# Layer 0's attention with scores in runs of nine over a ring of seven PSUM banks

## The chip, the cores and the metric

The kernel runs on one core of one Trainium2 chip. The metric is device time in microseconds for one launch. Five engines work side by side, each through its own queue in order: TensorE (PE) multiplies, ScalarE (ACT) takes exponentials and copies, VectorE (DVE) adds, GpSimd (POOL) and SyncE (SP) issue most DMAs. PE's results go to PSUM, which has eight banks of 512 fp32 per partition.

## The reference

Two layers on an image batch `x` of 2 x 256 x 64 x 64 in fp32. Layer 0 is attention over all 4096 pixels with 8 heads of 32 channels; layer 1 (local and strided attention and a 3x3 convolution) is not touched by the change.

```python
B, C, H, W = (2, 256, 64, 64)
NUM_HEADS = 8
qkv = jnp.einsum('bchw,oc->bohw', x, qkv_w) + qkv_b[None, :, None, None]
qkv = qkv.reshape(b, 3, num_heads, head_dim, n)
q, k, v = (qkv[:, 0], qkv[:, 1], qkv[:, 2])
attn_logits = jnp.einsum('bhci,bhcj->bhij', q, k) * scale
attn_weights = jax.nn.softmax(attn_logits, axis=-1)
out = jnp.einsum('bhij,bhcj->bhci', attn_weights, v)
...
x = x + _L0_conv_ref(_gn(x), L0_conv_qkv_w, L0_conv_qkv_b, 8)
x = x + _L1_conv_ref(_gn(x), ...)
```

## The kernel before

For each of the two images the kernel normalises `x`, projects queries, keys and values, runs layer 0's attention (`attention0`), and then layer 1. Only `attention0` changes.

**Units, blocks, groups.** A head's queries are cut in two halves of four tiles of 512; half a head is a group, so there are 16 groups. In a group `j` runs over 32 blocks of 128 keys, and a block has four units, one for each query tile. A unit is a matmul of 128 keys by 512 queries into one PSUM bank (the score, L505), followed by an exponential from that bank into a place of `es` (L511). An image has 16 x 32 x 4 = 2048 units. No maximum is subtracted; the sum of the exponentials is divided out at the end.

**Places.** The exponentials go round a ring of `RING` = 28 places of 512, the first `RING_A` = 17 in one tile and the rest in another, so a run of units is cut where places 17 and 28 begin. `at_places` does the cutting.

**Values.** For a block, `quarters` (L521) multiplies four units by the block's values; each unit makes 32 of the 128 output partitions of bank `av`. A block is worked in two half-blocks of 256 queries, but in one step at `j` = 0 and `j` = 31, so a group has 62 steps (`per_group`). One matmul shows as two records in the trace: a half-block has eight.

**Sums of the exponentials.** DVE adds each block's four units into `e` (L550, L558), except seven blocks a group (`SUMMED`), which POOL adds with accumulating DMAs (L566, L568). At the group's end the sums are joined (L748) and reduced over partitions by PE into a spare PSUM bank (`sum_rows`, called in `finish`), copied by ACT (L598) and sent off by SP.

**The loop.** PE, ACT and DVE run in the order in which the program is written (`manual_schedule`). A round of the loop calls `scores`, which takes seven units in three PSUM tiles, `sa` of three banks, `sb` of two and `sc` of two, and writes one exponential for each tile. Then come value steps of units that were scored in earlier rounds: `have` is the number of units before this call, `share` keeps the steps two behind their even share, `must` is the least number of blocks that have to be begun so that the places that the next call overwrites are free. When somebody wants a spare bank (`wanted`), `scores` uses two banks of `sa` and gives the third away; the row sum is then made after two steps (`here == 2`). A group's end closes the round, and ACT copies `av` (L762) so that the next group can begin.

The eight banks are thus three of `sa`, two of `sb`, two of `sc` and one of `av`. A tile of several banks is free for the next round when its exponential has read all of it.

Of the kernel before, what the change touches and what calls it, by code (L numbers as in the profile page):

```python
# [9 lines left out]
F32 = mybir.dt.float32  # L10
I32 = mybir.dt.int32
F32R = mybir.dt.float32r
AF = mybir.ActivationFunctionType
# [4 lines left out]
P = 128  # L18
B, C, H, W = 2, 256, 64, 64
N = H * W  # L20
T = 512
# [4 lines left out]
NH0 = C // HD0  # L26
# [14 lines left out]
def direct_layers(ctx: ExitStack, tc: tile.TileContext, a: dict, out: bass.AP, bad: bass.AP):  # L41
# [3 lines left out]
    nc = tc.nc  # L45
# [11 lines left out]
    psum = {}  # L57

    def w4(shape, name, dtype=F32):
        return work.tile(shape, dtype, tag="w4", name=name)  # L60
# [304 lines left out]
    SC0 = 1.0 / math.sqrt(HD0)  # L365
# [8 lines left out]
    NJ = N // P  # L374
# [77 lines left out]
    RING, RING_A = 28, 17  # L452
# [11 lines left out]
    def attention0(b, xts, held):  # L464
# [10 lines left out]
        n_units = NH0 * 2 * NJ * 4  # L475
# [4 lines left out]
        places = []  # L480
        n_places = 0

        def at_places(first, n):

            while n > 0:
                at = first % RING
                m = min(n, (RING_A if at < RING_A else RING) - at)
                yield m, es[:, at : at + m, :] if at < RING_A else held["es"][:, at - RING_A : at - RING_A + m, :]
                first, n = first + m, n - m

        def scores(spare):

            nonlocal n_places
            bank = None
            for tag, size in (("sa", 3), ("sb", 2), ("sc", 2)):
                first = len(places)
                n = min(size - (spare and size == 3), n_units - first)
                if n <= 0:
                    break
                sc = psum["sc"].tile([P, size, T], F32, tag=tag, name=f"{tag}_{b}_{first}")  # L500
                if spare and size == 3:
                    bank = sc[:, size - 1, :]
                for i in range(n):
                    g, (j, u) = (first + i) // (4 * NJ), divmod((first + i) % (4 * NJ), 4)
                    nc.tensor.matmul(  # L505
                        sc[:, i, :], held["k", g // 2][:, j * P : (j + 1) * P], held["q", g, u // 2][:, u % 2, :],
                        start=True, stop=True,
                    )
                i = 0
                for m, dst in at_places(n_places, n):  # L510
                    nc.scalar.activation(dst, sc[:, i : i + m, :], AF.Exp, scale=SC0)  # L511
                    i += m
                places.extend(range(n_places, n_places + n))
                n_places += size
            return bank

        def quarters(dst, lhs, rhs, start, stop, part=None):

# [17 lines left out]
        def add_rows(g, j):  # L536
            if j == 0:
                sums[g] = psum["sc"].tile([P, T], F32, tag="av", name=f"av_{b}_{g}")
                added[g] = [w4([P, 2, T], f"e_{b}_{g}_{w}") for w in range(2)]
                return  # L540
            for w in range(2):
                dst = added[g][w]
                if j in summed(g):
                    if w == 0:
                        add_in_memory(g, j)
                    continue
                if j == 1:
                    first = two_units(g, 0, w), two_units(g, 1, w)
                    if len(first[0]) == len(first[1]) == 1:
                        nc.vector.tensor_add(dst, first[0][0][1], first[1][0][1])  # L550
                    else:
                        for s in range(2):
                            nc.vector.tensor_add(dst[:, s, :], unit(g, 0, 2 * w + s), unit(g, 1, 2 * w + s))
                    continue
                for s, src in two_units(g, j, w):
                    if g == last and j in SUMMED_LAST:
                        continue
                    nc.vector.tensor_add(dst[:, s, :], dst[:, s, :], src)  # L558
# [11 lines left out]
        def work_of(g, j):  # L570


            if (g, j) < (last, NJ - 3):
                add_rows(g, j)
            for part in (None,) if j in (0, NJ - 1) else range(2):
                if part == 1:
                    yield
                quarters(
                    sums[g], held["v"][:, (g // 2) % 2, j, :], lambda u: unit(g, j, u), j == 0, j == NJ - 1, part
                )  # L580

        def sum_rows(g, rows):
            if g == last:
                for part in range(2):
                    for j in SUMMED_LAST:
                        quarters(rows, ones, lambda u: unit(g, j, u), j == SUMMED_LAST[0], False, part)
                    quarters(rows, ones, lambda u: acc[u], False, False, part)
                    quarters(rows, ones, lambda u: added[g][u // 2][:, u % 2, :], False, True, part)
                return
            quarters(rows, ones, lambda u: added[g][u // 2][:, u % 2, :], True, True)  # L590
# [140 lines left out]
        def steps():  # L731

            for done in range(NH0 * 2 * NJ):
                g, j = divmod(done, NJ)
                if (g, j) == (last, NJ - 3):
                    assert len(places) == n_units
                    held["rows"] = psum["sc"].tile([P, 3, T], F32, tag="sa", name=f"rows_{b}")[:, 2, :]
                    for i in (NJ - 3, NJ - 2, NJ - 1):
                        add_rows(g, i)
                    sum_rows(g, held["rows"])  # L740
                for _ in work_of(g, j):
                    yield done
                if g and j == 0:

                    for w in range(2):
                        dst = added[g - 1][w]
                        for s in range(2) if w == 0 else (slice(0, 2),):
                            nc.vector.tensor_add(dst[:, s, :], dst[:, s, :], acc[s] if w == 0 else pair)  # L748
                    waiting.clear()
                if g and j == 1:  # L750
                    wanted.append(late[0].send)
                if g and j in (9, 17):
                    next(late[0])
                for what in also.get((g, j), ()):
                    what()
                if j == 4 and g % 2 == 0 and g // 2 + 1 < NH0:
                    fetch_head(b, g // 2 + 1, held)
                if j == NJ - 1:
                    waiting.append(g)
                    avs = w4([P, 2, T], f"avs_{b}_{g}")  # L760
                    if g < last:
                        nc.scalar.copy(avs[:, 0, :], sums[g])  # L762
                    copied[g] = avs
                    late[:] = [finish(g)]
                    next(late[0])
                    if g + 2 < NH0 * 2:
                        fetch_queries(b, g + 2, held)
                yield done + 1

        E = mybir.EngineType  # L770
        with tc.manual_schedule(engines={E.PE, E.Activation, E.DVE}):

            per_group = 2 * NJ - 2
            work, begun, taken = steps(), 0, 0
            scores(False)
            final = False
            while not final:
                have = len(places)  # L780
                use = wanted.pop(0) if wanted else None
                bank = scores(use is not None)
                final = have == n_units
                ready = have // 4
                share = have * per_group // (4 * NJ) - 2

                must = sum(place < n_places + 7 - RING for place in places[: 4 * ready : 4])
                if must % NJ == 1:
                    must += 1
                assert must <= ready  # L790
                here = 0
                while begun < ready and (taken < share or begun < must or final or use is not None):
                    if use is not None and here == 2:
                        use(bank)
                        use = None
                        continue
                    here += 1
                    group = begun // NJ
                    begun = next(work)
                    taken += 1  # L800
                    if begun // NJ > group and begun >= must and not final and use is None:
                        break
                if use is not None:
                    use(bank)
            assert next(work, None) is None
            return *finish_last(last), st
# [585 lines left out]
    for b in range(B):  # L1392
        xts = x_first if b == 0 else ahead["xts"]
        w0 = w0_first if b == 0 else ahead["w0"]
        with tc.tile_pool(name=f"ps0_{b}", bufs=8, space=PSUM) as psum["ps"]:
# [7 lines left out]
            held = project0(b, xn, w0)  # L1403
# [571 lines left out]
```

## Time and profile before

| what | value |
|---|---|
| runs | 3115.47, 3118.44 and 3122.96 us, median 3118.44 |
| profiled execution: span, first to last instruction | 3116.4 us |
| profiled execution: time around the span | not given in the profile |
| PE matmul busy | 3031.2 us, 97% |
| DVE busy | 2467.0 us, 79% |
| ACT busy | 2313.6 us, 74% |
| POOL busy | 836.7 us, 27% |
| attention0, first image: first score burst to last | 118.4 to 1151.0 us |
| attention0, second image | 1666.3 to 2699.3 us |

How to read the profile: a group is a line, an engine and an operation with the tiles that it writes and reads; the arrow points to what is written. Matmuls are pipelined and overlap in the trace, so the distance from start to start says more of their cost than their length. PEld is the load of a matmul's stationary operand. In the timeline, rows of one group that follow each other are merged and counted. A number in square brackets is idle time of the engine before the row, and what ended it.

### The profile page before, as it was taken

Reading aid. Unit: us, or ns where it says so; the run is one execution under the profiler, and the core shown is the slowest. Engines: PE = TensorE matmul, PEld = TensorE weight load, DVE = VectorE, ACT = ScalarE, POOL = GpSimd, SP = SyncE. Lnnn points to the kernel's source line nnn. Section 1 sums busy time; section 2 is a strip of 40 time slices with the busy share of each in tenths; the row PEclk is TensorE's granted clock in tenths of the full one; section 3 lists DMA queues with packets and bytes.
Section 4 is the critical chain, followed back from the end, with each engine's and each line's share of the span. In section 5 each row is a group of like instructions: output and inputs, shape, how many; then the busy total and the mean of one; then the engine's idle time right before and its main releaser. Section 6 shows DMA issues by size and latency. Waiting matters only on the chain. (4 is left out here: it accounts for less than half of the span.)

```text
span 3116.4 us, 62659 instructions
## 1 busy us (share of the span) xinstructions
PE 3031.2 (97%) x25129; PEld 1830.6 (59%) x25129; DVE 2467.0 (79%) x3126; ACT 2313.6 (74%) x2436; POOL 836.7 (27%) x923
## 2 busy tenths in 40 slices
PE   6999999999999999999989999999999999999998
PEld 4555555555555556677755555555555555476765
DVE  4599989999899999856556998989989999834543
ACT  2699999999999984622237999999999999734333
POOL 2022222222222231055301222222222222305440
PEclk9999999999999999999999999999999999999999
DMA  7969679797897761230159687796888975700000
GB/s 241 270 132 185 143 150 172 154 178 150 164 181 154 145 133 33 75 134 29 41 193 268 128 176 151 156 176 138 177 162 164 181 153 123 170 4 4 21 14 22
DMA packets 243787, 424.41 MB, mean 136 GB/s; under 512 B 99112, under 2 KB 109916, under 8 KB 241308
## 3 DMA queue, kind: packets, MB, share of 16 engines
q0 software_dynamic: 94992, 238.36, 39.8%
q1 hardware_dynamic: 147580, 181.68, 21.6%
q8 instruction: 199, 3.26, 0.4%
q14 instruction: 104, 0.85, 0.1%
q10 hardware_dynamic: 912, 0.27, 0.0%
HBM read 119.03 MB, written 68.39 MB: 60 GB/s over the span
## 5 line engine op out<-in xcount | busy, mean ns | idle before, releaser
L558 DVE TENSOR_TENSOR e<-e,es 128x1024 f32<-128x1024 f32 (+1 forms) x956 | 1038.6, 1142 | 79.6 <-ACT es L511 77.9
L521 PE MATMUL av<-es,v 128*32 128x256 f32 (+1 forms) x9644 | 746.7, 390 | 0.0
L558 DVE TENSOR_TENSOR e<-e,v 128x1024 f32<-128x1024 f32 (+1 forms) x640 | 675.2, 1107 | 47.7 <-ACT v L511 46.6
L511 ACT ACTIVATE es<-sa 128x1536 f32<-128x1536 f32 (+1 forms) x444 | 635.7, 1432 | 93.1 <-PE sa L505 54.9
L505 PE MATMUL sa<-q,k 128*128 128x512 f32 x1736 | 561.4, 430 | 9.2 <-ACT avs L598 3.5
L521 PE MATMUL av<-v 128*32 128x256 f32 (+1 forms) x6228 | 506.5, 389 | 0.0
L521 PEld LDWEIGHTS av<-es,v 128*32 128x32 f32 x9644 | 316.1, 109 | 299.4 <-issue 160.6
L505 PEld LDWEIGHTS sa<-q,k 128*128 128x128 f32 x1736 | 280.0, 188 | 291.8 <-issue 135.4
L505 PE MATMUL sc<-q,k 128*128 128x512 f32 x1180 | 371.4, 396 | 1.7 <-ACT es L511 0.7
L505 PE MATMUL sb<-q,k 128*128 128x512 f32 x1180 | 371.0, 395 | 1.1 <-ACT es L511 1.1
L521 PEld LDWEIGHTS av<-v 128*32 128x32 f32 x6228 | 216.5, 109 | 178.6 <-issue 81.2
L511 ACT ACTIVATE es<-sc 128x1024 f32<-128x1024 f32 x296 | 306.9, 1037 | 0.0
L511 ACT ACTIVATE v<-sc 128x1024 f32<-128x1024 f32 x294 | 304.9, 1037 | 0.1
L511 ACT ACTIVATE es<-sb 128x1024 f32<-128x1024 f32 x296 | 302.0, 1020 | 3.8 <-DMA acc<-es 3.8
L511 ACT ACTIVATE v<-sb 128x1024 f32<-128x1024 f32 x294 | 300.0, 1020 | 0.0
L505 PEld LDWEIGHTS sb<-q,k 128*128 128x128 f32 x1180 | 221.2, 188 | 55.4 <-ACT es L511 2.9
L505 PEld LDWEIGHTS sc<-q,k 128*128 128x128 f32 x1180 | 210.5, 188 | 71.8 <-ACT es L511 12.1
L511 ACT ACTIVATE v<-sa 128x1536 f32<-128x1536 f32 (+1 forms) x146 | 209.2, 1433 | 35.6 <-PE sa L505 17.0
L948 PE MATMUL mm<-v,wf 128*128 128x256 f32 x1024 | 227.6, 380 | 1.5 <-DVE z L957 1.5
L568 POOL DMA_DIRECT2D es<-es x116 | 98.9, 853 | 475.6 <-ACT es L511 424.3
L948 PEld LDWEIGHTS mm<-v,wf 128*128 128x128 f32 x1024 | 193.3, 190 | 36.8 <-issue 9.9
L938 POOL TENSOR_TENSOR v<-col 128x512 f32<-128x512 f32 x128 | 165.1, 1316 | 179.2 <-ACT rk_sr L1089 39.2
(262 smaller groups left out, 3179.0 us busy)
## 6 DMA issues: line engine op xcount, KB each, us to landing
acc<-es POOLq DMA_DIRECT2D x128, 512.0 KB, 6.2
acc<-v POOLq DMA_DIRECT2D x84, 512.0 KB, 6.4
es<-es POOLq DMA_DIRECT2D x136, 256.0 KB, 4.5
v<-es POOLq DMA_DIRECT2D x132, 256.0 KB, 5.1
k<-wk_halves SPq DMA_DIRECT2D x64, 512.0 KB
q<-wq_halves SPq DMA_DIRECT2D x256, 128.0 KB
v<-v POOLq DMA_DIRECT2D x90, 256.0 KB, 5.4
es<-v POOLq DMA_DIRECT2D x86, 256.0 KB, 3.9
```

What stands on the lines that cost most here:

```text
L505: nc.tensor.matmul(sc[:, i, :], held["k", g // 2][:, j * P : (j + 1) * P], held["q", g, u // 2][:, u % 2, :], start=True, stop=True,)
L511: nc.scalar.activation(dst, sc[:, i : i + m, :], AF.Exp, scale=SC0)
L521: nc.tensor.matmul(dst[HD0 * u : HD0 * u + HD0, n], lhs, rhs(u)[:, n], start=start, stop=stop)
L558: nc.vector.tensor_add(dst[:, s, :], dst[:, s, :], src)
L568: nc.gpsimd.dma_start(out=dst, in_=src, accum_op=ALU.add)
L938: (nc.gpsimd.tensor_add if plus else nc.gpsimd.tensor_sub)(dst, rows(one), rows(two))
L948: nc.tensor.matmul(mm[:, m, r, :], wf[:, k, 4 * r + q, m * P : (m + 1) * P], v[r // 2][:, r % 2, k, :], start=k == 0, stop=k == KC - 1,)
```

## The change

The three PSUM tiles become one tile `ring` of seven banks, and a unit's bank is its place modulo seven. A call of `scores` takes nine units in runs of 1, 1, 3, 2 and 2 (`PHASE`), each with its own exponential; a run is also cut where the ring of banks or the ring of places wraps. So the eighth and ninth unit of a call use the banks of the first and second. A spare bank is the next one of the ring, taken after the nine, and skips a place as before. `have` now counts the units that lie at least seven behind the end of the call just made. `reach`, ten, takes the place of seven in `must`. A group's last two steps are worked in the round that reaches them (`ending`), and the last three blocks of all are held until all scores are made. The row bank of the last group comes from the ring, too.

```diff
-        def scores(spare):
+        BANKS = 7
+
+        PHASE = (1, 1, 3, 2, 2)
+        ring = psum["sc"].tile([P, BANKS, T], F32, tag="ring", name=f"ring_{b}")
+
+        def spare_bank():
 
             nonlocal n_places
-            bank = None
-            for tag, size in (("sa", 3), ("sb", 2), ("sc", 2)):
-                first = len(places)
-                n = min(size - (spare and size == 3), n_units - first)
-                if n <= 0:
-                    break
-                sc = psum["sc"].tile([P, size, T], F32, tag=tag, name=f"{tag}_{b}_{first}")
...
+            n_places += 1
+            return ring[:, (n_places - 1) % BANKS, :]
+
+        def runs_of(n):
+
+            at = n_places
+            while n > 0:
+                e = at % RING
+                m = min(n, BANKS - at % BANKS, (RING_A if e < RING_A else RING) - e)
+                yield at, m
+                at, n = at + m, n - m
+
+        def scores():
+
+            nonlocal n_places
+            for size in PHASE:
+                for at, m in list(runs_of(min(size, n_units - len(places)))):
+                    sc = ring[:, at % BANKS : at % BANKS + m, :]
+                    for i in range(m):
...
+                    ((_, dst),) = at_places(at, m)
+                    nc.scalar.activation(dst, sc, AF.Exp, scale=SC0)
+                    places.extend(range(at, at + m))
+                    n_places = at + m
...
-                    held["rows"] = psum["sc"].tile([P, 3, T], F32, tag="sa", name=f"rows_{b}")[:, 2, :]
+                    held["rows"] = spare_bank()
...
+            behind, reach = 7, sum(PHASE) + 1
             work, begun, taken = steps(), 0, 0
-            scores(False)
-            final = False
-            while not final:
-                have = len(places)
+            while begun < NH0 * 2 * NJ:
+                scores()
                 use = wanted.pop(0) if wanted else None
-                bank = scores(use is not None)
-                final = have == n_units
-                ready = have // 4
+                bank = spare_bank() if use is not None else None
+                final = len(places) == n_units
+                have = n_units if final else len(places) - behind
+                ready = max(0, have) // 4
                 share = have * per_group // (4 * NJ) - 2
 
-                must = sum(place < n_places + 7 - RING for place in places[: 4 * ready : 4])
+                must = sum(place < n_places + reach - RING for place in places[: 4 * ready : 4])
...
-                while begun < ready and (taken < share or begun < must or final or use is not None):
+                while begun < ready:
                     if use is not None and here == 2:
                         use(bank)
                         use = None
                         continue
+                    ending = taken % per_group >= per_group - 2
+                    if not (taken < share or ending or begun < must or final or use is not None):
+                        break
+                    if not final and begun == NH0 * 2 * NJ - 3:
+                        break
```

More of the change, by code (lines that the diff above doesn't have):

```diff
@@ L489, in at_places @@
                 first, n = first + m, n - m
-        def scores(spare):
+        BANKS = 7
+        PHASE = (1, 1, 3, 2, 2)
+        ring = psum["sc"].tile([P, BANKS, T], F32, tag="ring", name=f"ring_{b}")
+        def spare_bank():
             nonlocal n_places
-            bank = None
-            for tag, size in (("sa", 3), ("sb", 2), ("sc", 2)):
-                first = len(places)
-                n = min(size - (spare and size == 3), n_units - first)
-                if n <= 0:
-                    break
-                sc = psum["sc"].tile([P, size, T], F32, tag=tag, name=f"{tag}_{b}_{first}")
[L501 to L515, printed above, removed]
@@ new lines, in spare_bank @@
+            n_places += 1
[13 more added lines that the diff above has]
+                    for i in range(m):
+                        unit = len(places) + i
+                        g, (j, u) = unit // (4 * NJ), divmod(unit % (4 * NJ), 4)
+                        nc.tensor.matmul(
+                            sc[:, i, :], held["k", g // 2][:, j * P : (j + 1) * P], held["q", g, u // 2][:, u % 2, :],
+                            start=True, stop=True,
+                        )
+                    ((_, dst),) = at_places(at, m)
+                    nc.scalar.activation(dst, sc, AF.Exp, scale=SC0)
+                    places.extend(range(at, at + m))
+                    n_places = at + m
```

## The prediction

> **What bounds the kernel now.** I read the 40 slices first, then the busy time of the two stretches that the change lives in, then single rows of PE and ACT in them.
>
> ```profile
> PE   6999999999999999999989999999999999999998
> DVE  4599989999899999856556998989989999834543
> ACT  2699999999999984622237999999999999734333
> ```
>
> ```profile
> 118.40:1151.00 1032.60, 1027.90 (x10029) 584.73 (x10029) 946.83 (x967) 966.51 (x915) 276.23 (x338) 1.00 0.80 162
> 1666.30:2699.30 1033.00, 1027.79 (x10030) 584.12 (x10030) 947.07 (x967) 966.34 (x915) 272.70 (x338) 1.00 0.80 161
> ```
>
> Columns of the second view: stretch, us, then busy time of PE, weight loads, DVE, ACT, POOL. These are layer 0's attention for the two images: 1033 us each, two thirds of the span. PE has work in 99.5% of it, ACT in 94%, DVE in 92%. A busy PE says little by itself, so I look at how PE's time is made up. Two rounds of the loop in PE's timeline (start, duration, group):
>
> ```profile
> 602.91 0.98 PE L505 MATMUL sa<-q,k 128*128 128x512 f32 x3
> 603.73 0.63 PE L505 MATMUL sb<-q,k 128*128 128x512 f32 x2
> 604.20 0.62 PE L505 MATMUL sc<-q,k 128*128 128x512 f32 x2
> 604.75 1.50 PE L521 MATMUL av<-es,v 128*32 128x256 f32 x24
> 606.18 0.96 PE L505 MATMUL sa<-q,k 128*128 128x512 f32 x3
> ...
> 634.80 0.63 PE L505 MATMUL sc<-q,k 128*128 128x512 f32 x2
> 635.36 1.93 PE L521 MATMUL av<-es,v 128*32 128x256 f32 x32
> 637.23 0.50 PE L505 MATMUL sa<-q,k 128*128 128x512 f32 x1
> ```
>
> Starts tell more than durations, which overlap. Inside a burst a score costs 0.235 us (603.73 to 604.20 for two). Seven would be 1.645, but from the first score to the first value matmul pass 1.84: **0.195 more**. Values: 24 records take 1.43 (604.75 to 606.18), 32 take 1.87; the rest of the trace has 1.86, so eight (one half-block) cost 0.43 and three leave **0.14 over**. So a round of the loop costs about 0.335 us that belongs neither to a unit nor to a half-block. Check over a group of 128 units: 128 x 0.235 = 30.1; its 62 steps are 60 of 0.43 and two whole blocks of 0.86, 27.5; row sums 0.86 (646.18 to 648.91 in the trace, less its values); rounds 128/7 = 18.3 x 0.335 = 6.1. Sum 64.6, x 16 groups = 1033 us, which is the stretch. PE's own sequence explains all of it; waits are a few us. PE is the bound.
>
> ACT in the same place:
>
> ```profile
> 603.97 1.45 ACT L511 ACTIVATE es<-sa 128x1536 f32<-128x1536 f32 x1 [0.42 <-ACT es L511]
> 605.32 1.02 ACT L511 ACTIVATE v<-sb 128x1024 f32<-128x1024 f32 x1
> 606.22 1.03 ACT L511 ACTIVATE v<-sc 128x1024 f32<-128x1024 f32 x1
> ...
> 641.44 0.61 ACT L762 COPY avs<-av 128x512 f32<-128x512 f32 x1
> 641.92 1.49 ACT L511 ACTIVATE es<-sa 128x1536 f32<-128x1536 f32 x1
> ```
>
> Starts again: three banks hold ACT 1.35 us, two banks 0.90: 0.448 per bank and next to nothing per instruction. ACT is idle before the three-bank one, which is where it waits for PE's third score.
>
> **What the Trainium skill says.** *TensorEngine Tiling (Array Packing)*, Key Properties: changing the tiling mode drains the TensorE. Scores use 128*128, values 128*32, so each round switches twice; the 0.335 us agrees in kind, and the page has no figure. *ScalarE: Activation LUTs*, What ACT_TABLE_LOAD costs: an ACTIVATE with immediates takes 186 ns + 0.833 ns per element, and back-to-back ones overlap by about 93 ns. That gives an estimate of 1373 ns for 1536 elements and 946 for 1024; the trace has 1349 and 901, less per instruction than the page. *PSUM — Partial Sum Buffer*, bank collisions: guard PSUM by bank and quadrant, not by address. That is what lets a ring be handed over bank by bank; nothing in this trace shows it for PSUM.
>
> **The change, part by part.**
>
> *Nine scores a round.* The page counts 444 + 146 = 590 exponentials from `sa`, one a round: 295 rounds an image. With nine units it is 228 (227 x 9 + 5). Scores, value steps and row sums stay the same in number. 67 rounds fewer x 0.335 = 22.4 us an image, **45 us** in all. All of it lies on PE, which sets the end of the stretch. A half-block read as 0.44 instead of 0.43 leaves 0.305 a round, so 41 to 45.
>
> *Smaller exponentials.* Runs also break where the ring of seven ends and at places 17 and 28 of the 28 `es` places. Counting the loop gives 1298 exponentials an image: 696 of one bank, 454 of two, 148 of three, where there were about 885. No exponential of one bank is in the trace. Nearest row: L762's copy of one bank, which holds ACT 0.464 us at best (0.48 in the rows above). Below: 0.453 (the 0.448 slope and the 5 ns left); above: 186 + 427 - 93 = 520 ns by the skill's page. I take 0.464. ACT an image: 696 x 0.464 + 454 x 0.901 + 148 x 1.349 = 932, and 31 copies x 0.464 = 14: 946 us, against 937 before by the same reckoning. PE's stretch becomes 1010. ACT has 64 us to spare (25 at 0.520), so this costs nothing as long as PE covers it.
>
> *The ring's hand-over.* A round's clock on PE: scores start at 0, 0.34, 0.575, then every 0.235 to the ninth at 1.985; values at 2.31; next round at 2.31 + 4.36 x 0.43 + 0.14 = 4.33. An exponential starts 0.48 after its last score starts (603.49 to 603.97). So ACT: 0.48, 0.94, then 1.53 (its fifth score starts at 1.045), 2.87, 3.78, free at 4.68; the next round wants it at 4.33 + 0.48 = 4.81. Score 8 takes the bank of unit 1 (exponential ends 1.07, plus 0.15 as from L598's copy, ending 648.76, to the score at 648.91): 1.22 against its turn at 1.75. Score 9 takes that of unit 2: 1.68 against 1.985. Slack 0.3. All others take banks freed in the round before. A copy makes ACT 0.33 late once; score 9's slack just holds that. Behind a waiting score on PE stand the round's values, and behind those the next round.
>
> *Seven behind, `ending`, `break`.* By the same count twelve rounds an image have two or three half-blocks (3.4 to 3.8 us for ACT's 4.2), after which score 9 waits some 0.3: +4 us an image. Before has such rounds too (the seven scores that start at 383.28 take 2.18 us instead of 1.84), some 2 us. Net +2 an image.
>
> *Spare bank.* It moves from `sa`'s third bank, which the next round's first score waited for, to a place that is wanted seven scores on.
>
> ```profile
> PEld sa L505 <- ACT avs L598: 8.3, 15, 0.8
> PE sa L505 <- ACT avs L598: 1.7, 6, 0.3
> ```
>
> PE itself lost only 1.7 us an image: -2. The row sum now needs the three-bank exponential of its own round (ends 2.98, +0.15) at 2.31 + 0.86 = 3.17: free, or 0.2 x 17 = 3 us an image if ACT is late. L598's copy and the DMAs that SP issues behind it (L599, L601) move by under a round; what reads them is asked for eight blocks, some 15 us, later.
>
> *DVE, POOL, SP.* The same adds, accumulating DMAs and fetches, in a stretch 2% shorter: DVE 947 of 1010. An `es` place comes round after 28 x 0.481 = 13.5 us instead of 13.8; the accumulating DMAs land 6.2 to 6.4 us after issue, and ACT waited 5.6 us in all for them. 0 to +4.
>
> Sum: -45 + 4 - 4 + 2 = -43. The profiled span is 3116.4, 2 us below the median of 3118.44; what lies around the span isn't shown, so I carry the difference over: **3075 us**.
>
> **Rivals.** (1) *ACT becomes the bound, slower.* If a lone bank doesn't overlap its neighbour because each waits for its own score, it holds ACT for the record of a copy, 0.585, and 0.07 for the semaphore: 696 x 0.655 + 409 + 200 + 14 = 1079 an image, some 46 more than now: 3210. ACT passes PE from 0.55 a bank and the old time from 0.58. Against it: L762's 0.46 to 0.48, and that the next instruction is usually ready. (2) *The hand-over eats the gain.* If score 9 waits in every round, 22.4/228 = 0.1 us is break-even: 3118. For it: ACT's spare 0.13 a round is thin, and lateness is carried on until a longer round. Against it: the 0.3 slack. Half eaten is 3095. (3) *Not bank by bank.* If the ring, one tile, were tracked whole, each of five runs would wait for the one before: 5 x 0.63 + 4.7 of exponentials + 2.0 of values is 9.9 a round, 5.6 ms in all. Against it: DVE reads places of the one tile `es` while ACT writes others. (4) *More gained:* start-up (4 us over the sum at 118) and end-of-stage waits shrink too: 3062.
>
> **How the numbers follow.** Forecast and (4) 0.71, its own range 3062 to 3090; half eaten 0.09; (2) in full 0.09, of it 0.02 beyond break-even; (1) 0.08; (3) 0.03. About 0.2% (6 us) can be told from no change. Faster 0.80, within 0.07, slower 0.13. Range 3060 to 3110: it takes in 0.520 a bank (ACT 986 and some 10 us of waits) and the half-eaten case.
>
> **What would show it.** PE's score bursts: nine starts 0.235 apart, ending 2.3 us after the first; 455 rounds; stretches of about 1011 us; one-bank exponentials 0.46 apart; hardly any wait of `ring` scores for ACT. Wrong if score starts 8 and 9 show gaps of 0.1 or more in most rounds, or ACT is busy throughout while PE waits.

## The result and the profile after

The changed kernel takes **6914.75 us** (four runs, 6914.57 to 6915.9); the kernel before takes 3119.19 in the same comparison. The ratio is 2.2172, with an interval of 2.2140 to 2.2203. The prediction said 3075, with a range of 3060 to 3110: a small gain was forecast, and the kernel takes over twice as long.

The same 40 slices as before, now over a span of 6914.0 us, with the granted TensorE clock as the last row:

```profile
PE   7666666666666666679986666666666666666799
DVE  3333333333333333347543333333333333333344
ACT  3333333333333333334233333333333333333333
PEclk8666666666666666679986666666666666666799
```

In layer 0's attention no engine is full any more: PE has work in six or seven tenths, ACT and DVE in three. The rest of the program lies mainly in slices 19 to 21 and the last two, where PE is nearly full as before. In the kernel before, the last row was 9 in every slice:

```profile
PEclk9999999999999999999999999999999999999999
```

The busy times of the two attention stretches, same columns as before (stretch, us, PE, weight loads, DVE, ACT, POOL, granted clock, DMA share, GB/s). The windows are some 50 and 40 us wider than the stretches:

```profile
118.00:3100.00 2982.00, 1989.44 (x10384) 811.43 (x10384) 1040.25 (x1063) 1134.05 (x1363) 291.49 (x351) 0.65 0.28 57
3560.00:6530.00 2970.00, 1977.33 (x10240) 800.07 (x10242) 1025.94 (x1005) 1130.94 (x1352) 282.53 (x345) 0.65 0.29 59
```

From the first score burst to the last, the stretch took 1032.6 and 1033.0 us before and takes 2929.3 and 2927.7 now: 1897 and 1895 us more, 3791 of the 3798 by which the profiled span grew. So the whole loss lies in attention0. Within the stretches ACT's work grew from 966 to 1110 us an image, and it is far from full. PE isn't full either: this is a stretch that waits. Who waits for whom (engine, tile and line that waits, the releaser, total us, times, longest):

```profile
ACT es L525 <- PE ring L520: 2100.2, 1554, 4.4
PE ring L520 <- ACT es L525: 1200.8, 1296, 1.6
...
ACT v L525 <- PE ring L520: 1359.6, 1005, 5.0
...
PE ring L520 <- ACT v L525: 767.1, 844, 1.9
```

PE's scores waited for ACT's exponentials 2140 times and ACT's exponentials for PE's scores 2559 times. The page counts 2596 exponentials. Nearly every exponential waits for its score, and most score runs wait for an exponential: the two engines take turns. One round in the timeline shows it at the level of single instructions:

```profile
901.66 0.50 PE L520 MATMUL ring<-q,k 128*128 128x512 f32 x1
...
902.20 0.60 ACT L525 ACTIVATE v<-ring 128x512 f32<-128x512 f32 x1 [2.72 <-PE ring L520]
...
902.85 0.50 PE L520 MATMUL ring<-q,k 128*128 128x512 f32 x1 [0.69 <-ACT v L525]
...
903.39 0.60 ACT L525 ACTIVATE v<-ring 128x512 f32<-128x512 f32 x1 [0.59 <-PE ring L520]
...
904.04 1.06 PE L520 MATMUL ring<-q,k 128*128 128x512 f32 x3 [0.69 <-ACT v L525]
...
905.19 1.45 ACT L525 ACTIVATE v<-ring 128x1536 f32<-128x1536 f32 x1 [1.20 <-PE ring L520]
...
906.69 1.22 PE L520 MATMUL ring<-q,k 128*128 128x512 f32 x2 [1.59 <-ACT v L525]
...
907.95 1.02 ACT L525 ACTIVATE v<-ring 128x1024 f32<-128x1024 f32 x1 [1.31 <-PE ring L520]
...
909.02 1.22 PE L520 MATMUL ring<-q,k 128*128 128x512 f32 x2 [1.11 <-ACT v L525]
...
910.18 3.19 PE L533 MATMUL av<-es,v 128*32 128x256 f32 x25
```

Read the ends. The first exponential ends at 902.20 + 0.60 = 902.80, and the next score, into another bank, starts at 902.85. The second ends at 903.99, the next score starts at 904.04; the third at 906.64 and 906.69; the fourth at 908.97 and 909.02. Every run of scores starts 0.05 us after the exponential of the run before has ended, although that exponential reads a bank which the new scores don't touch. The trace has 2142 places where one run of scores follows another within a round, and in every one of them the distance is 0.051 to 0.053 us. The next round begins at 913.75, 12.09 us after this one.

Summed over an image (226 intervals between rounds in the trace): from a round's first score to its first value matmul 9.21 us on average, from there to the next round 3.75. (9.21 + 3.75) x 226 = 2929, which is the stretch. Without waits and at full clock the first part would be 9 x 0.235 + 0.195 = 2.31, and the second some 2.1.

### The profile page after: what moved, and what is told of

The parts are those of the page before. It is cut to its first block, busy times and chain, and to the rows that moved or that the text cites. A ratio compares the mean times of both kernels' runs of the same rounds, so it can differ in the third digit from the quotient of the medians.

```text
span 6914.0 us, 63839 instructions
## 1 busy us (share of the span) xinstructions
PE 4868.0 (70%) x25129; PEld 2231.9 (32%) x25129; DVE 2577.0 (37%) x3122; ACT 2599.5 (38%) x3262; POOL 835.4 (12%) x923
## 5 line engine op out<-in xcount | busy, mean ns | idle before, releaser
L520 PE MATMUL ring<-q,k 128*128 128x512 f32 x4096 | 2232.2, 613 | 1971.4 <-ACT es L525 1200.8
L525 ACT ACTIVATE es<-ring 128x512 f32<-128x512 f32 (+2 forms) x1572 | 1335.0, 849 | 2103.0 <-PE ring L520 2100.2
L520 PEld LDWEIGHTS ring<-q,k 128*128 128x128 f32 x4096 | 900.2, 251 | 3299.1 <-ACT es L525 1812.6
L525 ACT ACTIVATE v<-ring 128x512 f32<-128x512 f32 (+2 forms) x1024 | 855.7, 836 | 1364.0 <-PE ring L520 1359.6
L533 PE MATMUL av<-es,v 128*32 128x256 f32 (+1 forms) x9684 | 1242.7, 601 | 0.0
L533 PE MATMUL av<-v 128*32 128x256 f32 (+1 forms) x6188 | 851.8, 601 | 0.0
L533 PEld LDWEIGHTS av<-es,v 128*32 128x32 f32 x9684 | 467.7, 162 | 603.3 <-issue 584.9
L533 PEld LDWEIGHTS av<-v 128*32 128x32 f32 x6188 | 317.5, 162 | 378.1 <-issue 366.4
L580 POOL DMA_DIRECT2D acc<-es x118 | 104.7, 887 | 209.6 <-ACT es L525 185.7
L580 POOL DMA_DIRECT2D v<-es x112 | 109.5, 977 | 94.4 <-ACT es L525 93.0
```

The costliest lines, as they stand in the source:

```text
L520: nc.tensor.matmul(sc[:, i, :], held["k", g // 2][:, j * P : (j + 1) * P], held["q", g, u // 2][:, u % 2, :], start=True, stop=True,)
L525: nc.scalar.activation(dst, sc, AF.Exp, scale=SC0)
L533: nc.tensor.matmul(dst[HD0 * u : HD0 * u + HD0, n], lhs, rhs(u)[:, n], start=start, stop=stop)
L580: nc.gpsimd.dma_start(out=dst, in_=src, accum_op=ALU.add)
```

## The experiments

Two questions: what makes PE and ACT take turns, and, if that is taken away, is the predicted gain there? Where the table has a ratio, it is to the kernel before in the same comparison; kernels without one ran once.

| run | PSUM tiles for scores | scores a round | us | ratio |
|---|---|---|---|---|
| e1 | seven of one bank | 9 | 3117.69 | 1.0003 (0.9994 to 1.0011) |
| e2 | one of seven banks, kernel before | 7 | 5870.93 | |
| e3 | one of six banks | 9 | 7008.13 | |
| e4 | as e3, with filler matmuls | 9 | 6227.49 | |
| e5 | 1, 1, 2 and 3 banks | 8 | 3120.22 | 1.0002 (0.9994 to 1.0011) |
| e6 | 1, 1, 1, 2 and 2 banks | 9 | 3107.74 | 0.9962 (0.9948 to 0.9975) |
| e7 | seven of one bank | 7 | 3100.30 | 0.9939 (0.9924 to 0.9954) |
| e8 | two, of 4 and 3 banks | 9 | 5688.73 | |
| e9 | seven of one bank | 8 | 3098.89 | 0.9946 (0.9930 to 0.9963) |
| e10 | 3, 2 and 2 banks, kernel before with the new pacing | 7 | 3122.42 | 1.0024 (1.0014 to 1.0034) |

### e1: the ring as seven tiles of one bank

Everything else of the change stays, but each exponential reads one bank.

```diff
-        PHASE = (1, 1, 3, 2, 2)
-        ring = psum["sc"].tile([P, BANKS, T], F32, tag="ring", name=f"ring_{b}")
+        PHASE = (1,) * 9
+        ring = [psum["sc"].tile([P, T], F32, tag=f"ring{i}", name=f"ring_{b}_{i}") for i in range(BANKS)]
...
-                    sc = ring[:, at % BANKS : at % BANKS + m, :]
+                    sc = ring[at % BANKS]
```

> Rounds of nine as in the change, but the ring is seven tiles of one bank each and every exponential takes one bank. Theory A (the ring as one tile is handed over whole, so every run of scores waits for the exponential before it, and the idle PE then gets half its clock): no such wait is left, PE bounds again, 228 rounds an image instead of 295 at 0.335 us, 3075 us (3060 to 3095). Theory B (rounds of nine with short exponentials are slow in themselves, because a lone bank costs ACT much more than 0.46 us or because score 8 and 9 wait): over 3200, up to the change's 6914.

Measured: 3117.69 us, no difference from before that can be told. The 3.8 ms are gone, and so is the clock's fall (mean 0.992). So nothing in the change's order, pacing or number of exponentials costs those milliseconds. But the 45 us of the prediction, and with them the expected 3075, aren't there either. The stretches take 1030.2 and 1036.0 us, where PE's own sum, by the prediction's prices with the 226 rounds, is 1005. (The prediction's sums, 1033 before and 1010 after, take in all units and steps of an image. A stretch ends where its last round begins, and what comes behind that is worth some 6 us. All sums from here on leave it out; that of the kernel before is then 1027.) ACT's own timeline in this kernel tells why:

```profile
963.38 5.50 ACT L525 ACTIVATE es<-ring 128x512 f32<-128x512 f32 x11
968.64 3.68 ACT L525 ACTIVATE v<-ring 128x512 f32<-128x512 f32 x7
```

Eleven exponentials of one bank in 968.64 - 963.38 = 5.26 us: 0.478 each. Over all 4014 that follow another one without idle time the mean is 0.488, because some 70 an image take 0.1 to 0.5 us longer. 2048 x 0.49 and the copies, about 15 us, make 1018 us: ACT is nearly full (it is idle for 10 and 16 us in the two stretches), and in some 120 of the 226 rounds the scores that take the banks of the first and second unit of their own round, or the value matmul behind them, come late, mostly by 0.05 to 0.6 us; all this lateness sums to 23 and 27 us in the two images. That is the 25 to 31 us between stretch and sum, within what the sum can be trusted for.

### e2: the kernel before with one tile of seven banks

Rounds of seven, runs of 3, 2 and 2, pacing and the spare bank stay as before; only the three tiles become slices of one.

```diff
-            for tag, size in (("sa", 3), ("sb", 2), ("sc", 2)):
+            for at, size in ((0, 3), (3, 2), (5, 2)):
...
-                sc = psum["sc"].tile([P, size, T], F32, tag=tag, name=f"{tag}_{b}_{first}")
+                sc = whole[:, at : at + size, :]
```

> The kernel before with one edit: sa, sb and sc are slices of one tile of seven banks. Rounds of seven and the sizes 3, 2, 2 stay. Theory A: sb waits for sa's exponential and sc for sb's. At full clock a round is 6.5 us instead of 3.49, about 4880 us in all; at half clock in most of it 8.2, about 5870. So 4800 to 6000, and a granted clock well under 1. Theory B: 3119, as before.

Measured: 5870.93 us at a mean clock of 0.802. Two runs in its timeline:

```profile
911.17 0.73 PE L507 MATMUL whole<-q,k 128*128 128x512 f32 x2 [1.54 <-ACT es L513]
...
912.00 1.02 ACT L513 ACTIVATE es<-whole 128x1024 f32<-128x1024 f32 x1 [0.88 <-PE whole L507]
913.08 0.74 PE L507 MATMUL whole<-q,k 128*128 128x512 f32 x2 [1.17 <-ACT es L513]
```

The exponential ends at 913.02 and the scores of the next two banks start at 913.08. Each bank is used exactly as in the kernel before; only the tile that it belongs to is another. One tile alone turns 3117 us into 5871. So **the tile is handed over whole**. One thing more differs: the one tile is made once an image, while the kernel before makes its three anew in every round. That isn't the cause, since e1's seven tiles are also made once an image.

### e8: two tiles, of four and three banks

```diff
-        ring = psum["sc"].tile([P, BANKS, T], F32, tag="ring", name=f"ring_{b}")
+        CUT = 4
+        ring = [
+            psum["sc"].tile([P, n, T], F32, tag=f"ring{i}", name=f"ring_{b}_{i}") for i, n in enumerate((CUT, BANKS - CUT))
+        ]
```

A run is also cut where the second tile begins.

> The change with the ring cut into a tile of four banks and one of three, runs cut there too. Theory A: a run waits only for the last exponential of its own tile, so about half of the waits stand behind an exponential that is already done: between 4000 and 5800, and a clock between 0.7 and 1. If something other than the tile made the runs wait (the order of ACT, the places of es): 6900 or more, since there are more runs.

Measured: 5688.73 us, mean clock 0.800, a round 10.2 us in the median where it was 12.9 with one tile. Two tiles give back some 1226 us. One round shows both kinds of hand-over:

```profile
905.75 0.49 PE L528 MATMUL ring<-q,k 128*128 128x512 f32 x1
906.28 0.60 ACT L533 ACTIVATE v<-ring 128x512 f32<-128x512 f32 x1 [3.85 <-PE ring L528]
906.93 1.20 PE L528 MATMUL ring<-q,k 128*128 128x512 f32 x4 [0.69 <-ACT v L533]
907.47 0.60 ACT L533 ACTIVATE v<-ring 128x512 f32<-128x512 f32 x1 [0.59 <-PE ring L528]
908.22 1.45 ACT L533 ACTIVATE es<-ring 128x1536 f32<-128x1536 f32 x1
...
909.72 0.73 PE L528 MATMUL ring<-q,k 128*128 128x512 f32 x2 [1.59 <-ACT es L533]
```

The score at 905.75 and the first of the four at 906.93 lie in the second tile, and the latter starts 0.05 us after the exponential's end at 906.88. The other three of the four lie in the first tile; they follow at once, before the exponential of the score ahead of them has even begun (907.47). At 909.72 the first tile is wanted again, 0.05 us after its exponential has ended.

When the ring is followed through the whole trace, 1360 runs lie in the tile of the run before them in their round, and every one starts 0.053 to 0.054 us after that run's exponential has ended. 1042 lie in the other tile, and every one starts 0.79 to 1.70 us before that end. So it is not the order of ACT, and not the place in `es`, that makes a run wait, but the tile. As over half of the neighbours share a tile, an image still loses 1008 us between first scores and first values against the full pace.

### e3 and e4: what the half clock costs

e3 only sets `BANKS = 6`, which frees a bank. e4 is e3 and puts, behind each run of m scores, 2 + 2m further score matmuls into that free bank, which nothing reads.

```diff
-        BANKS = 7
+        BANKS = 6
+        junk = psum["sc"].tile([P, T], F32, tag="junk", name=f"junk_{b}")
...
+                    for _ in range(2 + 2 * m):
+                        nc.tensor.matmul(
+                            junk, held["k", g // 2][:, j * P : (j + 1) * P], held["q", g, u // 2][:, u % 2, :],
+                            start=True, stop=True,
+                        )
```

> The change with a ring of six banks, as the base for the next kernel: 1337 instead of 1298 runs an image. Theory A: a run waits for the run before it whatever the size of the ring, so 39 runs more an image at 1.2 us: 7010 (6900 to 7100). Theory B (the ring is too short for nine): clearly slower, over 7300.

> The same with PE kept busy: after each run of m scores 2 + 2m more score matmuls of the same operands into the free bank, which nobody reads. They fit in the wait. Theory A, with the half clock as a second cause: PE gets its full clock, values take 2.0 us a round instead of 3.7 and a round about 10 instead of 13: 5610 (5500 to 6000), though PE does over twice the matmuls. If the half clock were only a companion of the waits: 7010 or more, and values still 3.7 us.

Measured: 7008.13 and 6227.49 us. The first stretch of e3, then of e4 (columns as above):

```profile
118.00:3100.00 2982.00, 1983.29 (x10089) 793.48 (x10092) 1010.16 (x974) 1121.22 (x1374) 275.33 (x338) 0.64 0.28 56
```

```profile
118.00:2700.00 2582.00, 2581.53 (x16738) 1784.13 (x16739) 1006.76 (x972) 1118.88 (x1366) 275.63 (x338) 1.00 0.32 65
```

With more for PE to do the kernel is 781 us faster. PE is busy throughout, the clock is whole again, and the values of a round are back at some 2.1 us. The taking of turns stays: from a round's first score to its first value matmul an image still loses 1580 us against the full pace, where e3 loses 1590. The saving is smaller than expected. The end of a round in e4's timeline gives a reason:

```profile
901.63 0.42 PE L522 MATMUL ring<-q,k 128*128 128x512 f32 x1
...
901.89 1.09 PE L527 MATMUL junk<-q,k 128*128 128x512 f32 x4
...
902.91 0.40 PE L540 MATMUL av<-es,v 128*32 128x256 f32 x1
```

The values stand behind the fillers of the last run, where nothing has to be bridged: four of them here, and in all four in 98 rounds and six in 356, which at 0.235 us each make 594 us. Runs also start 0.13 us after the exponential before them where e3 has 0.05, which in 2220 places makes some 177 us. An estimate without both is 5450, at the lower end of what was expected. So 781 us is what the half clock costs at least.

### e5 and e6: runs of mixed sizes with hand-over by small tiles

These come nearest to what the prediction assumed: fewer and longer rounds with some exponentials of several banks, and each tile belonging to one run. e5 takes eight scores in runs of 1, 2, 1, 3 and 1 (the last takes the first one's bank again), e6 nine in runs of 1, 1, 2, 2, 1, 1 and 1. The core of e6:

```diff
+            order = [(one[0], 1), (one[1], 1), (pairs[0], 2), (pairs[1], 2), (one[2], 1), (one[0], 1)]
+            order += [] if spare else [(one[1], 1)]
+            singles[:] = [one[2], one[0], one[1]]
```

> Rounds of eight with each tile handed over whole and still early enough: two tiles of one bank, one of two, one of three, runs 1, 2, 1, 3 and again 1 in the first tile; the two single tiles change places each round. 258 rounds an image instead of 295, 5 exponentials in a round. Theory A (PE's 0.335 us a round is real; e1 gave nothing because 2048 lone banks at 0.49 us are 1018 us of ACT an image): ACT is 258 x 3.72 = 960 us, PE bounds, 37 x 0.335 = 12 us an image less: 3093 (3085 to 3105). Theory C (PE's cost of a round isn't saved, whatever ACT does): 3118.

> Rounds of nine in the same way: three tiles of one bank, two of two, runs 1, 1, 2, 2, 1 and again 1, 1 in the first two tiles, the single tiles rotating. 230 rounds an image, ACT 230 x 4.25 + 15 = 993 us, PE 1011. Theory A: 22 us an image less, 3075, or up to 3095 as ACT is only 2% short of PE. Theory C: 3118.

e5: 3120.22 us, nothing gained, where 3093 was expected. Its median round of 3.91 us has no wait (the prices give 3.94), so a round does cost what it should, but 16 to 17 us an image of late scores come in 34 rounds. Some 28 of these follow a round that was shorter by a half-block or more, and are mostly 0.25 to 0.4 us late, 9 to 10 us in all. Behind some of the longer waits stand DMAs:

```profile
ACT v L515 <- DMA acc<-v: 9.1, 4, 4.4
ACT es L515 <- DMA acc<-es: 5.3, 3, 2.4
```

ACT waited for accumulating DMAs that still read the places it wanted to write, and the scores behind it waited too: 14 us in both images together, so this is a part of the loss only. That these waits grow because the round is worked in another order is argued, not shown.

e6: 3107.74 us, 0.4% faster than before, where 3075 to 3095 was expected. PE's own sum is 1006 us an image, the stretches take 1028.2 and 1026.9. Late scores make 14 to 15 us of the difference, in 126 rounds of the first image at 0.05 to 0.3 us each; the remaining 7 or so I didn't follow.

### e7 and e9: seven and eight scores a round over one-bank tiles

As e1, with `PHASE = (1,) * 7` and `(1,) * 8`.

> As e1, but in rounds of seven: the same 2048 lone exponentials an image, 293 rounds. Theory A (ACT bounds both): as e1, 3118 to 3130. If PE bounded e1 and rounds of nine saved their 45 us there, but something else lost it: 3150 to 3165.

> Seven tiles of one bank, lone exponentials, rounds of eight: between e7 (rounds of seven, PE never waits, 1025 us an image) and e1 (rounds of nine, 25 us of waits an image at scores 8 and 9). PE's own sum is 257 x 0.335 instead of 291 x 0.335, 11 us an image less than e7; ACT's 2048 x 0.49 + 15 is 1018. If ACT's total is what limits e1, this lands at 1018 to 1024 an image, 3086 to 3098 in all. If score 8 waits as scores 8 and 9 do in e1, no better than e7: 3100 to 3110.

Measured: 3100.30 and 3098.89 us, 0.6% and 0.5% faster than before, and no difference between the two that can be told. e7 misses both of its expectations, e9 falls between its two. In e7 no score matmul waits for ACT, and the stretches take 1025.0 and 1025.3 us against PE's sum of 1027; the kernel before is 6 us above its own sum of 1027. What e7 gains is these 6 us; 2 to 3 of them are late scores, the rest wasn't followed. PE is its bound, but ACT is level with it, idle for only 5 to 6 us in each stretch. At eight the sum is 1013, but the stretches are 1023 and 1021, with 6 to 8 us of late scores, and ACT is idle for 6 to 7 us in each: there ACT sets the pace. Between seven and nine, what a round saves on PE comes back as waits for ACT. These two beat both kernels.

### e10: the pacing alone

The kernel before with its three tiles, and `behind`, `ending` and the hold-back of the last three blocks from the change.

```diff
+            behind, reach = 7, 7
...
+                have = n_units if final else len(places) - behind
...
+                    ending = taken % per_group >= per_group - 2
```

> The kernel before with the change's pacing alone (values counted seven behind the call just made, `ending`, the last three blocks held back); sa, sb, sc and the spare bank in sa stay, and so do rounds of seven. It tells where e7's 19 us come from. If the pacing makes them: 3100 to 3106. If they come from handing over one bank at a time and from the spare bank that no longer costs a score: 3114 to 3120.

Measured: 3122.42 us, 0.24% slower (0.14 to 0.34%), above both expectations. Its stretches are 3 us an image longer than before's. So e7's gain doesn't come from the pacing but from what else e7 has: tiles of one bank with an exponential each, and the spare bank that goes with them. Which of these makes it was not tried.

## Why the prediction was wrong

**The step that failed** is "The ring's hand-over". It let a bank go back to PE as soon as its own exponential had ended, and gave score 9 a slack of 0.3 us. The runs show the tile as the unit: e2 only makes the three tiles one and pays 2.75 ms; e1 takes the one tile away and pays nothing; in e8 a run waits for the exponential before it in all 1360 places where both share a tile, and in none of the 1042 where they don't. The support was an inference from another memory: DVE reads places of the one tile `es` while ACT writes others. That is so for `es` in SBUF, and it doesn't carry over to a PSUM tile in this program. The prediction also leaned on *PSUM — Partial Sum Buffer*, bank collisions, of the Trainium skill: guard by bank and quadrant. That says what the hardware needs, not what a program waits for, and here it waited for more. The kernel before held a warning. When `sa` gives its third bank to a row sum, the next round's first score goes into the first bank of `sa`, while ACT's copy may still read the third. One of these places:

```profile
585.77 0.97 PE L505 MATMUL sa<-q,k 128*128 128x512 f32 x3 [0.27 <-ACT avs L598]
```

The copy ends at 585.72. PE stood idle for it in 12 of 30 such rounds and started 0.05 us after its end, although it was to write another bank. `sa` is made anew each round there, so this is a hint and no proof. The prediction named this very wait under "Spare bank", drew nothing from it for the ring, and wrote that nothing in the trace shows a hand-over by bank in PSUM. (Its 0.15 us for a hand-over is from a round in which PE still had values to do.) With so little evidence on the one point that everything rested on, 0.03 for the third rival was far too little.

**Rival (3)** had the mechanism: 9.9 us a round, 5.6 ms. Measured are 12.96 and 6.9 ms, for two reasons. A round has 1298 / 228 = 5.7 runs, not five, since runs are cut at the rings' ends (the prediction's own count). And the clock: values took 3.75 us where it had 2.0. In the six-bank pair the clock is worth at least 781 us. *TensorE: Matmul & The Clock Gate*, A second HAM failure mode: psum-queue depth-cycling, of the Trainium skill, describes the like in another kernel: short idle times between groups of matmuls make the granted clock go back and forth between 4/8 and 8/8. The trace agrees: the recorded clock of the stretches alternates between 0.5 and 1.0 and takes no other value.

**Nine scores a round.** The price of 0.335 us a round holds: e7's stretches are within 2 us of the sum with it, and e1 and e6 are their sums and their late scores to within 8 us. That it comes from the change of tiling mode, no run here shows. But the gain isn't to be had whole: e6, nearest to the prediction's picture, kept 12 us of 45.

**Smaller exponentials.** The number is exact: the trace has 2596 for two images, 1392 of one bank, 908 of two, 296 of three, twice the counts given. The price of a lone bank was too low: 0.478 and, on average, 0.488 in e1 instead of 0.464. The page *ScalarE: Activation LUTs*, What ACT_TABLE_LOAD costs, gave an estimate of 0.520, too high. At 0.49, for 696 lone banks 0.026 more is 18 us an image for ACT: not yet the bound in the change's mix (946 + 18 against 1010), but 18 / 228 = 0.08 of the 0.13 us that ACT had to spare a round, on which the hand-over lives.

**Rival (2)**, the gain eaten by score 9, is what e1 shows, though with lone exponentials only: ratio 1.0003, with the gaps at the scores that it named. e6 is between it and the forecast. **Rival (1)**, ACT as the bound, did not happen. Its cause did: in the change a lone exponential waits for its own score and holds ACT for 0.597 us (mean of 1392), but ACT has long pauses there.

**Pacing and spare bank.** Net +2 an image was for the pacing; e10 measures +3 with rounds of seven. The spare bank's -2 fits e7, where such waits are gone, but wasn't tried by itself.

**Left open.** Exponentials of several banks over tiles of one bank each were not tried, so how the change itself would run if its ring were handed over bank by bank can only be judged by e1 and e6; it was not measured.

## What to carry to other kernels

Before a change lets two runs share a PSUM tile, look in a trace for a place where one engine writes a part of such a tile while another reads a different part; in the kernel before, the row sum in `sa` was such a place. If there is none, give each run its own tile or price the wait as the likeliest case. When PE and ACT take turns, PE pays twice: for the wait, and for its own slower clock afterwards. And where three engines are within a tenth of each other, a fixed cost saved on the first is worth no more than the room that the second has left: price the second at its average over a long stretch, not at its best.

## What the runs showed of the hardware

The granted clock fell to half although PE never paused for long: in the round shown, idle times were 0.69 to 1.59 us, one after another, no wait of a score for ACT was longer than 1.9 us, and the mean clock of the stretch was 0.65. Matmuls whose result nobody reads, placed in those idle times, brought it to 1.00 and made the kernel 781 us faster, though they delay other work (e3 to e4). Two engines handing a bank to each other lose little in between: 0.05 us from the end of an exponential to the next score's start, and, for a lone score, 0.54 from its start to its exponential's where the recorded clock is 1.0, 0.83 where it is 0.5 (medians in the changed kernel).
